# The end of a convolution, attention and expert kernel: a copy moved inside a merge, a last selection in another order, expert turns and output sums regrouped

## Chip, cores and metric

The kernel runs on one core of one Trainium2 chip. The metric is the device time of one execution in microseconds; all data are 32-bit floats. The program holds a fast path and a general path that is taken only when a check of value ranges fails; with the inputs used here the fast path alone is executed.

## The reference, cut to what matters

The input `x` has 4 images of 128 channels and 64 x 64 places. Layer 0 normalises groups of channels, takes three 1x1 convolutions with a leaky rectifier, and attends every place to every other (4096 x 4096 per image). Layer 1 sees the places as 4096 tokens of 128 features: a running-softmax attention with 8 heads, and then experts that choose their tokens.

```python
x = x + _L0_conv_ref(_gn(x), ...)            # layer 0
t = _to_tokens(x)
t = t + _L1_attn_ref(_ln_t(t), W_kv, q_proj) # running softmax over earlier tokens
t = t + _L1_ffn_ref(_ln_t(t), ...)           # 64 experts
x = _from_tokens(t, x)

def _L1_ffn_ref(x, gate_w, gate_b, weight1, weight2):
    logits = jnp.einsum('bsd,ed->bse', x, gate_w) + gate_b
    probs = jax.nn.softmax(logits, axis=1)               # over the tokens
    vals, idx = jax.lax.top_k(probs.transpose(0, 2, 1), 8)
    ...
    pooled = jnp.einsum('bked,bke->bed', gathered, topv) # 8 tokens per expert and image
    h = gelu(pooled @ weight1)                           # with a bias row
    out = h @ weight2                                    # with a bias row
    weighted = jnp.einsum('beo,bke->bkeo', out, topv)
    ...
    outputs = outputs.at[jnp.arange(Bn)[:, None], flat_idx].add(weighted)
```

For each image, each of the 64 experts picks the 8 tokens with the largest gate values; their weighted sum goes through the expert once, and the result is added to the same 8 tokens with the same weights. So the experts cannot start before the last token of an image has passed its gate.

## The kernel before

The residual stream lives in SBUF as `t`, with tokens on the partitions: 32 blocks of 512 tokens, 8 blocks per image. `layer0` does the convolutions and the large attention, `loop` the running attention in 32 steps, with a slot plan (`make_plan`) that places gate work between the matmuls of a step: slots 1, "V", 2, "W", "D", 3, 4, "O", "T", "G" in this order. The orders of TensorE, ScalarE (ACT), VectorE (DVE) and GpSimd (POOL) are as written in the program in this part; the DMAs that are named here are issued on SP's queue, the gathers on POOL's.

The change touches only the end of it.

**Last step of the loop (block 31).** `totals` forms sums over tokens in the PSUM tile `f_pt`; `close_totals` (L1166) copies it to SBUF on DVE; `outputs` (L1180) multiplies with that copy and adds to `t`. In slot "O", ahead of the last `totals` and of `close_totals`, the plan puts `merge_halves(3, 1)`, the first gather, `old_exps` and `root_table`. `merge_halves` (L1346) takes the best candidates of image 3 from the blocks done so far: values to the top 8, then for each of 4 ranks a comparison of places, a product with the row numbers and a sum (`f_rowf`), which becomes the row to gather. `root_table` (L1248) is a tiny square root that brings in ACT's table ahead of need.

**`last_choice` (L1514).** Block 31 alone is not yet in the choice. Its statistics, root, normalised rows (`f_x`), their transposes (`gate_turn`, `f_gtr`), logits (`f_pl`) and best 8 per half follow each other; then the new best are merged with the old top 8 (`f_pw1`, `f_merged`, `f_top`), exponentials are taken (`f_ce`, `chd`), the candidates are weighed and spread over experts (`weigh_candidates`, `spread_candidates`, `f_dd`), and TensorE sums into `f_pp`: four products with the gathered rows (L1576) and four with the tokens of block 31 (L1594), which need the transposed selection from `f_pc`. `f_pr` brings the divisors to every partition, and the last multiplication (L1605) fills `env.pooled`. Between these steps stand *fillers*: `fill(n, tag)` (L1467) transposes block `n` of `t` to PSUM, and `put_back(n, copy, count)` (L1480) copies it over the tokens in `t`, here always on ACT, since the output wants channels on partitions. Blocks 0 to 9 are turned in this way. The PSUM buffers go by tag: "kv" has two of two banks, "t", "o", "x" and "sm" one each.

**`experts` (L1700).** 64 experts in 16 groups of 4. For group `g`: `first(g)` (L1730) multiplies `env.pooled` by the first weights into `f_ph` and copies to `f_hr` on ACT; `turn(g)` (L1743) transposes that (`f_htr`, tag "sm"), adds the bias on DVE and takes the gelu on ACT into one of two `f_hs` tiles; `second(g)` (L1759) multiplies with the second weights into `f_eo`. As soon as `first` and `second` have read the weights of an expert, the DMA of a later expert into the same place is issued (`reload1`, L1672, and `reload2`, L1679). Beside it `turn_back(n)` (L1692) turns the remaining blocks of `t`. After 8 and 16 groups `spread` (L1775) takes the sums back to one row per expert and image: four products to one tile `f_pe` and four steps on DVE to `env.eo`.

**`stores` (L1814).** For two blocks at a time the outputs of the experts are spread over the tokens (`f_sct`, L1820), added to `t` on DVE, for every third pair with half of it on ACT and POOL, and written out, 512 KB at a time, the first and last pair in two parts of 256 KB.

Of the kernel before, what the change touches and what calls it, by code (L numbers as in the profile page):

```python
# [8 lines left out]
F32 = mybir.dt.float32  # L9
# [8 lines left out]
def conv_attn_hybrid_kernel(  # L18
# [809 lines left out]
    def fast():  # L828
# [418 lines left out]

        def root_table():  # L1248
            nc.scalar.activation(env.gnb[:, 0, 0:1], eps5, AF.Sqrt)
# [96 lines left out]
        def merge_halves(b, columns=4):  # L1346
# [16 lines left out]
            for h in range(2):  # L1363
                half = slice(h * E, (h + 1) * E)
                nc.vector.tensor_copy(own[half], first8[half, :, 4 * h : 4 * h + 4])
            hit = room[:, 4 * w : 12 * w].rearrange("p (k j) -> p k j", k=4)
# [147 lines left out]
        def last_choice():  # L1514
# [6 lines left out]
            fill(1, "kv", 1)  # L1521
            row_numbers(b, 1, 2)
# [9 lines left out]
            put_back(0, act, 2)  # L1532
# [42 lines left out]
            for kk in range(4):  # L1575
# [6 lines left out]
            )  # L1582
            ct = ex_at(1)[:, HB:].rearrange("p (j x) -> p j x", j=2)
# [8 lines left out]
            for h in range(2):  # L1592
# [5 lines left out]
                if h == 0:  # L1598
                    pr = ps.tile([P, BLK], F32, tag="t", name="f_pr3")
# [100 lines left out]
        def experts():  # L1700
# [74 lines left out]
            def spread(half, add):  # L1775
                pe = ps.tile([P, B, C], F32, tag="t", name=f"f_pe_{half}")
                for b in range(B):
                    at = 32 - 32 * half
                    nc.tensor.matmul(
                        pe[:, b, :], z_at[b][:, at : at + P], env.swap, start=True, stop=True,  # L1780
                    )
                for b in range(B):
                    nc.vector.scalar_tensor_tensor(
                        out=env.eo[:, b, :], in0=pe[:, b, :], scalar=env.den[:, b : b + 1],
# [29 lines left out]
        def stores():  # L1814
            for n in range(0, NB, 2):
                b, k = blocks[n]
                sc = ps.tile([P, 2, BLK], F32, tag="kv", name=f"f_sct_{n}", bufs=2)
                for h in range(2):
                    half = slice(h * E, (h + 1) * E)
                    nc.tensor.matmul(  # L1820
                        sc[:, h, :], env.eo[half, b, :],
                        env.lg[b][half, k : k + 2, :].rearrange("p k x -> p (k x)"),
                        start=True, stop=True,
                    )
                scv = sc.rearrange("p h (k x) -> p k h x", k=2)
                at = bass.ds(n * CPB, 2 * CPB)
                view = t[:, at, :].rearrange("p (k h c) x -> p k h (c x)", k=2, h=2)
                ends = n == 0 or n == NB - 2
                if n // 2 % 3 == 1:
                    part = env.rest.tile([P, 2, HB], F32, tag="xl", name=f"f_scs_{n}", bufs=3)  # L1830
                    nc.scalar.copy(part, scv[:, 0])
                    nc.gpsimd.tensor_tensor(view[:, 0], view[:, 0], part, ALU.add)
                    nc.vector.tensor_add(view[:, 1], view[:, 1], scv[:, 1])
                elif ends:
# [571 lines left out]
```

## Time and profile before

| | |
|---|---|
| runs shown | 2310.31, 2310.56, 2311.30 us (median 2310.56) |
| the profiled execution | 2303.66 us, of it 2301.8 us from first to last instruction |
| PE busy | 2238.5 us (97%) |
| DVE, ACT, POOL busy | 1447.1, 1092.2, 174.4 us |
| mean granted TensorE clock | 0.995 |
| read from HBM, written | 78.55 MB, 17.04 MB |
| start of `last_choice` on PE | about 2189.6 us after the start |
| start of `first(0)` | 2203.56 us |
| last group's `second` ends | about 2270.7 us |
| first store issued | 2274.57 us |

All positions in time are microseconds from the first instruction of the profiled execution. The durations of the profile belong to that one execution, which was shorter than the timed ones. "issue" in the chain of waits is time in which the engine that is on the chain waited for nothing that the profile shows. A matmul of 32-bit floats appears as two records, so counts of PE rows are twice those in the code where it isn't a transpose.

### The profile page before, as it was taken

Reading aid. Unit: us, or ns where it says so; the run is one execution under the profiler, and the core shown is the slowest. Engines: PE = TensorE matmul, PEld = TensorE weight load, DVE = VectorE, ACT = ScalarE, POOL = GpSimd, SP = SyncE. Lnnn points to the kernel's source line nnn. Section 1 sums busy time; section 2 is a strip of 40 time slices with the busy share of each in tenths; the row PEclk is TensorE's granted clock in tenths of the full one; section 3 lists DMA queues with packets and bytes.
Section 4 is the critical chain, followed back from the end, with each engine's and each line's share of the span. In section 5 each row is a group of like instructions: output and inputs, shape, how many; then the busy total and the mean of one; then the engine's idle time right before and its main releaser. Section 6 shows DMA issues by size and latency. Waiting matters only on the chain.

```text
span 2301.8 us, 43187 instructions
## 1 busy us (share of the span) xinstructions
PE 2238.5 (97%) x18352; PEld 1163.8 (51%) x18352; DVE 1447.1 (63%) x2380; ACT 1092.2 (47%) x1328; POOL 174.4 (8%) x380
## 2 busy tenths in 40 slices
PE   7999999999999999999999999999999999999997
PEld 3644444444444444444444444456556555566663
DVE  7666565655666565556555666667867777875643
ACT  2343334433333443344445554445566676565751
POOL 0000000000000000000000000011121121222311
PEclk9999999999999999999999999999999999999999
DMA  2000010000010000001000000020211211213488
GB/s 76 33 12 16 10 45 9 17 9 9 11 52 9 9 12 13 9 9 44 9 5 5 5 5 10 5 50 26 66 44 40 65 52 41 59 55 116 138 322 302
DMA packets 78555, 104.77 MB, mean 46 GB/s; under 512 B 8976, under 2 KB 44816, under 8 KB 78352
## 3 DMA queue, kind: packets, MB, share of 16 engines
q1 hardware_dynamic: 77264, 99.81, 13.9%
q8 instruction: 146, 2.39, 0.4%
q0 software_dynamic: 512, 1.05, 0.2%
q10 hardware_dynamic: 576, 1.05, 0.1%
q14 instruction: 57, 0.47, 0.1%
HBM read 78.55 MB, written 17.04 MB: 42 GB/s over the span
## 4 chain that ended last, share of the span: by engine, by line
PE 87%; DVE 6%; ACT 3%; DMA 2%; issue 1%; SPq 0%; POOL 0%; ACTq 0%; DVEq 0%; POOLq 0%
PE av L2009 37%; PE sc L1984 18%; PE f_pv L1128 9%; PE f_pk L973 8%; PE f_pt L1151 3%; PE f_po L1174 2%; PE pd L2035 1%; PE f_po L1186 1%; ACT f_e1a L980 1%; PE pa L1957 1%; DMA x<-in_x_dram 1%; PE pe L1931 1%; DVE f_e1a L981 1%; DVE f_e1a L982 1%; PE f_pl L1294 1%
## 5 line engine op out<-in xcount | busy, mean ns | idle before, releaser
L2009 PE MATMUL av<-pr,am 64*128 64x512 f32 x4096 | 977.7, 592 | 2.4 <-ACT pr L1989 2.4
L1989 ACT ACTIVATE pr<-sc 128x1024 f32<-128x1024 f32 x512 | 524.1, 1024 | 781.2 <-PE sc L1984 766.9
L1996 DVE TENSOR_TENSOR acc<-acc,pr 128x1024 f32<-128x1024 f32 x480 | 586.6, 1222 | 484.8 <-ACT pr L1989 480.5
L2009 PEld LDWEIGHTS av<-pr,am 64*128 64x128 f32 x4096 | 401.8, 187 | 472.9 <-issue 458.1
L1984 PE MATMUL sc<-e,e 64*128 64x512 f32 x2048 | 534.9, 591 | 3.3 <-DMA e<-side 3.3
L1984 PEld LDWEIGHTS sc<-e,e 64*128 64x128 f32 x2048 | 201.5, 187 | 234.7 <-issue 229.2
L1128 PE MATMUL f_pv<-f_held,f_ama 128*32 128x256 f32 x4096 | 237.5, 381 | 6.1 <-ACT f_e1a L980 5.1
L973 PE MATMUL f_pk<-f_held,f_ama 128*128 128x512 f32 x512 | 234.9, 603 | 0.0
L1133 ACT ACTIVATE f_amb<-f_pv 128x1024 f32<-128x1024 f32 x128 | 131.1, 1025 | 130.1 <-PE f_pv L1128 129.4
L981 DVE TENSOR_TENSOR f_e1a<-f_e1a,f_held 128x1024 f32<-128x1024 f32 x128 | 156.9, 1226 | 48.6 <-ACT f_e1a L980 48.3
L980 ACT ACTIVATE f_e1a<-f_pk 128x1024 f32<-128x1024 f32 x128 | 129.8, 1025 | 110.3 <-PE f_pk L973 56.1
L1128 PEld LDWEIGHTS f_pv<-f_held,f_ama 128*32 128x32 f32 x4096 | 129.2, 110 | 100.7 <-ACT f_e1a L980 11.9
L982 DVE TENSOR_REDUCE f_e1a<-f_e1a 128x8 f32<-128x1024 f32 x128 | 155.2, 1217 | 3.5
L973 PEld LDWEIGHTS f_pk<-f_held,f_ama 128*128 128x128 f32 x512 | 92.5, 190 | 108.3 <-issue 101.1
L1092 POOL COPY f_held<-f_e1a 32x32 f32<-32x32 f32 x128 | 30.7, 240 | 909.8 <-DVE f_e1a L1074 564.1
L1151 PE MATMUL f_pt<-f_amb,f_held 128*32 128x128 f32 x1920 | 83.2, 276 | 0.8 <-ACT f_amb L1133 0.8
L918 POOL MEMSET f_held<- 128x1024 f32 x1 | 1.0, 957 | 1036.6 <-DVE xn L1922 1036.6
L1151 PEld LDWEIGHTS f_pt<-f_amb,f_held 128*32 128x32 f32 x1920 | 60.0, 109 | 10.4 <-issue 5.2
L1192 DVE TENSOR_TENSOR t<-t,f_po 128x512 f32<-128x512 f32 (+1 forms) x33 | 22.1, 671 | 56.0 <-PE f_po L1186 56.0
L956 ACT ACTIVATE f_xl<-t,ln_nb,ln_rs 128x128 f32<-128x128 f32 x128 | 52.8, 491 | 0.8 <-PE pa L1957 0.8
L1275 ACT ACTIVATE f_x<-t,f_gnb,f_grs 128x128 f32<-128x128 f32 x122 | 49.7, 482 | 0.4 <-DVE f_gnb L1254 0.4
L1993 DVE COPY acc<-pr 128x1024 f32<-128x1024 f32 x32 | 22.2, 694 | 39.3 <-ACT pr L1989 39.3
(300 smaller groups left out, 1797.8 us busy)
## 6 DMA issues: line engine op xcount, KB each, us to landing
f_e2a<-f_rd SPq DMA_DIRECT2D x128, 128.0 KB, 2.9
xr<-in_xtok_dram SPq DMA_DIRECT2D x32, 256.0 KB, 3.0
f_table<-f_x SPq DMA_DIRECT2D x62, 128.0 KB, 2.0
out_dram<-t SPq DMA_DIRECT2D x14, 512.0 KB, 3.8
x<-in_x_dram SPq DMA_DIRECT2D x12, 512.0 KB, 6.4
e<-e SPq DMA_DIRECT2D x32, 128.0 KB, 2.2
f_ama<-f_rd SPq DMA_DIRECT2D x16, 256.0 KB, 3.8
f_e1b<-f_rd SPq DMA_DIRECT2D x16, 256.0 KB, 6.0
```

Of the source, the lines that this page charges most:

```text
L956: nc.scalar.activation(xl[:, c, :], t[:, b * NCH + i, :], AF.Identity, bias=ln_nb[:, b, i : i + 1], scale=ln_rs[:, b, i : i + 1],)
L973: nc.tensor.matmul(pk[:, i, :], xt_at(n)[:, bass.ts(c, P)], env.wks[:, bass.ts(i, BLK)], start=True, stop=True,)
L980: nc.scalar.activation(flat, pk.rearrange("p i x -> p (i x)"), AF.Silu)
L981: nc.vector.tensor_mul(ks, ks, env.qb)
L982: nc.vector.tensor_reduce(s[:, (n % GB) * CPB + c, :], ks, AX.X, ALU.add)
L1128: nc.tensor.matmul(pv[a * CH : (a + 1) * CH, i, :], xt_at(m)[:, bass.ts(c * NA + i, CH)], env.wvs[:, bass.ts(a, HH * C)], start=True, stop ...
L1133: nc.scalar.activation(env.amb[:, bass.ts(c, HD)], pv.rearrange("p i x -> p (i x)"), AF.Silu)
L1151: nc.tensor.matmul(env.pt[i * CH : (i + 1) * CH, :], lhs, rhs, start=i not in env.begun, stop=False, skip_group_check=True,)
L1984: nc.tensor.matmul(sc[:, u, :], e2[halves[u], p, :], e1[halves[u], cols], start=True, stop=True,)
L1989: nc.scalar.activation(pr, sc, AF.Exp)
L1996: nc.vector.tensor_add(acc, acc, pr)
L2009: nc.tensor.matmul(av, am[h, j, :], pr[h, u, :], start=(j == 0), stop=(j == NCH - 1))
```

## The change

1. The merge of slot "O" is cut in two: `merge_values` (up to the ranks' values and places) stays in "O", `merge_rows` and the first gather move to slot "T", behind `close_totals`.
2. In `last_choice`: the put-back of blocks 0 and 1 moves from behind `gate_norm` to the start. A new `exp_table`, a tiny exponential, follows the put-back of blocks 2 and 3; behind it stand the put-backs of blocks 4 and 5, which were after the exponentials. The filler of block 8 moves ahead of `f_pw1`, and blocks 10 and 11 become fillers too (tags "t" and "o"), put back where 4 and 5 were. `f_dd` is formed in two halves; the products with the gathered rows are cut in two pairs, the second behind `f_pc`; `f_pr` takes the last quarter of the tile of `f_pc`.
3. In `experts`: `turn(15)` moves ahead of `late_choice`, `turn_back` and `second` of group 14. Turning back starts with block 12, and two blocks per group are turned in groups 0 to 3 only (before: 0 to 5).
4. `spread` takes four tiles of 128 x 128 with the tags "t", "x", "sm", "t", and each product is followed by its step on DVE.
5. `stores`: for the first and the last pair the products are made per block (128 x 256, four of them) rather than per half (128 x 512, two).

```diff
+        def exp_table():
+            nc.scalar.activation(env.gnb[:, 0, 0:1], eps5, AF.Exp)
...
-        def merge_halves(b, columns=4):
+        def merge_halves(b):
+            merge_values(b)
+            merge_rows(b, 4)
+
+        def merge_values(b):
...
+            st["merge"] = (w, room, rows_)
+
+        def merge_rows(b, columns):
...
-        def spread_candidates(cw):
+        def spread_candidates(cw, parts=1):
             dd = ex_at(0)[:, : 4 * E].rearrange("p (k e) -> p k e", k=4)
-            nc.vector.tensor_tensor(
-                dd, env.pair[:, :E].unsqueeze(1).to_broadcast([P, 4, E]),
-                cw.unsqueeze(2).to_broadcast([P, 4, E]), ALU.mult,
-            )
+            m = 4 // parts
+            for i in range(parts):
+                nc.vector.tensor_tensor(
+                    dd[:, bass.ts(i, m)], env.pair[:, :E].unsqueeze(1).to_broadcast([P, m, E]),
+                    cw[:, bass.ts(i, m)].unsqueeze(2).to_broadcast([P, m, E]), ALU.mult,
+                )
             return dd
...
             fill(0, "kv")
             fill(1, "kv", 1)
+            put_back(0, act, 2)
             row_numbers(b, 1, 2)
             gathers(b, 1, 2)
             pool(B - 2)
...
             gathers(b, 2, 3)
-            put_back(0, act, 2)
             gate_turn(m, dve)
             row_numbers(b, 3, 4)
             gathers(b, 3, 4)
             put_back(2, act, 2)
+            exp_table()
+            put_back(4, act)
+            put_back(5, act)
             fill(6, "kv")
             gate_logits(m)
             fill(7, "kv", 1)
+            fill(8, "kv")
             late = st["cand"][:, bass.ts(k, 8)]
             pw = both_halves(late, "f_pw1")
-            fill(8, "kv")
             fill(9, "kv", 1)
+            fill(10, "t")
+            fill(11, "o")
...
             put_back(6, act, 2)
-            put_back(4, act)
             put_back(8, act, 2)
-            put_back(5, act)
-            dd = spread_candidates(weigh_candidates(b))
+            put_back(10, act)
+            put_back(11, act)
+            dd = spread_candidates(weigh_candidates(b), 2)
...
-            for kk in range(4):
+            for kk in range(2):
                 nc.tensor.matmul(pp, g_at(b, kk), dd[:, kk, :], start=(kk == 0), stop=False)
...
+            for kk in range(2, 4):
+                nc.tensor.matmul(pp, g_at(b, kk), dd[:, kk, :], start=False, stop=False)
...
-                    pr = ps.tile([P, BLK], F32, tag="t", name="f_pr3")
+                    pr = pc[:, 3 * P :]
...
             def spread(half, add):
-                pe = ps.tile([P, B, C], F32, tag="t", name=f"f_pe_{half}")
                 for b in range(B):
+                    pe = ps.tile([P, C], F32, tag=("t", "x", "sm", "t")[b], name=f"f_pe_{half}_{b}")
...
-            n = 10
+            n = 12
             for g in range(EG):
-                turn(g)
+                if g + 1 < EG:
+                    turn(g)
+                if g + 2 == EG:
+                    turn(g + 1)
                 late_choice(g)
-                for _ in range(2 if g < NB - 10 - EG else 1):
+                for _ in range(2 if g < NB - 12 - EG else 1):
...
+                if ends:
                     for i in range(2):
-                        nc.vector.tensor_add(view[:, i], view[:, i], scv[:, i])
+                        for h in range(2):
+                            half = slice(h * E, (h + 1) * E)
+                            nc.tensor.matmul(
+                                sc[:, h, bass.ts(i, HB)], env.eo[half, b, :],
+                                env.lg[b][half, k + i, :], start=True, stop=True,
+                            )
+                    view = t[:, at, :].rearrange("p (k h c) x -> p k h (c x)", k=2, h=2)
+                    for i in range(2):
+                        nc.vector.tensor_add(view[:, i], view[:, i], sc[:, :, bass.ts(i, HB)])
...
-            at(end, "O", merge_halves, B - 1, 1)
-            at(end, "O", gathers, B - 1, 0, 1)
+            at(end, "O", merge_values, B - 1)
+            at(end, "T", merge_rows, B - 1, 1)
+            at(end, "T", gathers, B - 1, 0, 1)
             at(end, "O", old_exps)
             at(end, "O", root_table)
```

More of the change, by code (lines that the diff above doesn't have):

```diff
@@ L1365, in merge_halves @@
                 nc.vector.tensor_copy(own[half], first8[half, :, 4 * h : 4 * h + 4])
+            st["merge"] = (w, room, rows_)
+        def merge_rows(b, columns):
+            st = sel[b]
+            own, top = st["own"], st["top"]
+            w, room, rows_ = st["merge"]
             hit = room[:, 4 * w : 12 * w].rearrange("p (k j) -> p k j", k=4)
@@ L1775, in spread @@
             def spread(half, add):
-                pe = ps.tile([P, B, C], F32, tag="t", name=f"f_pe_{half}")
                 for b in range(B):
+                    pe = ps.tile([P, C], F32, tag=("t", "x", "sm", "t")[b], name=f"f_pe_{half}_{b}")
                     at = 32 - 32 * half
                     nc.tensor.matmul(
-                        pe[:, b, :], z_at[b][:, at : at + P], env.swap, start=True, stop=True,
+                        pe, z_at[b][:, at : at + P], env.swap, start=True, stop=True,
                     )
-                for b in range(B):
                     nc.vector.scalar_tensor_tensor(
-                        out=env.eo[:, b, :], in0=pe[:, b, :], scalar=env.den[:, b : b + 1],
+                        out=env.eo[:, b, :], in0=pe, scalar=env.den[:, b : b + 1],
                         in1=add[:, b, :], op0=ALU.mult, op1=ALU.add,
@@ L1817, in stores @@
                 sc = ps.tile([P, 2, BLK], F32, tag="kv", name=f"f_sct_{n}", bufs=2)
[L1818 to L1825, printed above, removed]
-                at = bass.ds(n * CPB, 2 * CPB)
@@ L1827, in stores @@
[L1827 to L1834, printed above, removed]
-                    for i in range(2):
-                        nc.vector.tensor_add(view[:, i], view[:, i], scv[:, i])
-                else:
-                    nc.vector.tensor_add(view, view, scv)
+                ends = n == 0 or n == NB - 2
@@ new lines, in stores @@
+                at = bass.ds(n * CPB, 2 * CPB)
+                if ends:
+                    for i in range(2):
+                        for h in range(2):
[7 more added lines that the diff above has]
+                        nc.vector.tensor_add(view[:, i], view[:, i], sc[:, :, bass.ts(i, HB)])
+                else:
+                    for h in range(2):
+                        half = slice(h * E, (h + 1) * E)
+                        nc.tensor.matmul(
+                            sc[:, h, :], env.eo[half, b, :],
+                            env.lg[b][half, k : k + 2, :].rearrange("p k x -> p (k x)"),
+                            start=True, stop=True,
+                        )
+                    scv = sc.rearrange("p h (k x) -> p k h x", k=2)
+                    view = t[:, at, :].rearrange("p (k h c) x -> p k h (c x)", k=2, h=2)
+                    if n // 2 % 3 == 1:
+                        part = env.rest.tile([P, 2, HB], F32, tag="xl", name=f"f_scs_{n}", bufs=3)
+                        nc.scalar.copy(part, scv[:, 0])
+                        nc.gpsimd.tensor_tensor(view[:, 0], view[:, 0], part, ALU.add)
+                        nc.vector.tensor_add(view[:, 1], view[:, 1], scv[:, 1])
+                    else:
+                        nc.vector.tensor_add(view, view, scv)
```

## The prediction

> **What bounds the kernel now.** The page's slices come first: PE is busy in nearly all of them, but the change only touches the last 115 us, and there the DMA row rises to 8.
>
> ```profile
> PE   7999999999999999999999999999999999999997
> DMA  2000010000010000001000000020211211213488
> ```
>
> So I read the end by itself: the busy time of stretches cut where the DMA rate changes (columns: stretch, length, busy us of PE, PEld, DVE, ACT, POOL, then PE clock, DMA share, GB/s).
>
> ```profile
> 2184.00:2197.00 13.00, 10.88 (x196) 8.75 (x188) 7.44 (x35) 9.82 (x12) 3.79 (x4) 1.00 0.91 347
> 2197.00:2202.00 5.00, 3.34 (x32) 3.05 (x33) 2.82 (x14) 3.66 (x9) 0.00 (x0) 1.00 0.17 32
> 2203.50:2206.50 3.00, 2.94 (x16) 0.60 (x16) 0.00 (x1) 0.59 (x1) 0.00 (x0) 0.50 0.04 16
> 2206.50:2212.00 5.50, 5.50 (x61) 3.91 (x58) 2.88 (x9) 3.67 (x6) 0.28 (x2) 0.76 0.93 279
> 2212.00:2268.00 56.00, 51.60 (x694) 32.94 (x693) 12.60 (x37) 20.64 (x46) 4.19 (x25) 0.97 1.03 376
> 2268.00:2275.00 7.00, 5.52 (x56) 3.40 (x56) 2.82 (x8) 0.99 (x3) 0.00 (x0) 1.00 0.02 8
> 2282.00:2297.00 15.00, 9.60 (x36) 2.41 (x32) 9.98 (x11) 1.76 (x3) 3.82 (x3) 0.92 1.02 399
> ```
>
> The reader sees two full stretches of DMA and two empty ones. 2206.5 to 2268 is expert weights: 21 of the 64 experts are loaded ahead, and 43 x 512 KB = 22.5 MB follow, each load waiting until `first` or `second` has read the weights in its place. 2282 to 2297 is output. A stage that DMA fills moves as a whole with its first transfer; what PE and DVE do beside it costs nothing. So the time is set by the chain to the first reload (2205.50) and the chain from the last weights to the first stores. That is where I read the chain of waits (start, us, what):
>
> ```profile
> 2187.53 1.10 issue
> 2188.63 1.35 PE f_po L1186 x32
> ...
> 2194.96 0.66 PE f_etb L1476 x4
> 2195.62 0.61 PE f_pl L1294 x4
> ...
> 2198.78 0.79 issue
> 2199.57 1.08 PE f_pp L1576 x8
> 2200.65 0.23 PE f_pc L1579 x2
> ...
> 2201.51 0.66 PE f_pp L1594 x4
> ...
> 2203.56 3.64 PE f_ph L1735 x16
> ...
> 2271.04 1.17 PE f_pe L1779 x8
> 2272.24 0.36 DVE f_e1b L1783
> 2272.64 1.15 PE f_sct L1820 x4
> 2273.82 1.30 DVE t L1836 x2
> ```
>
> PE stands idle twice (1.10 and 0.79), and `first(0)` and `first(1)` take 3.64 where later pairs of groups take 2 x 1.00. The cause of the latter is the clock: cut at 3.41 us, it is 0.50 in 2202.33 to 2209.16 and 1.00 on both sides.
>
> [...] the changes at 2202.3, 2209.1, 2222.8 and 2226.2 lie 2, 4 and 1 windows of 3.41 apart, and a 128x32 by 512 f_ph matmul takes 1.06 slow, 0.62 fast. [...] The trace shows 1.28, and the ACTIVATE 0.01 later at 2186.39[...], so I use 1.28. [...] Here traffic ends at 2268.2 and PE gets the last weights at 2269.60, some 1.4 later.
>
> **The change, part by part.**
>
> *Totals copy inside the merge.* DVE copies f_pt (L1168) at 2188.24, behind five merge steps from 2187.13 on, while PE has ended its products at 2187.53. Moved ahead of those steps the copy runs 2187.13 to 2187.41; its matmuls ended at 2186.2. PE gains 2188.63 - 2187.55 = **1.08**, and the chain through t, statistics, root, norm and turn follows. POOL's first gather moves back behind the copy by 0.3; nobody reads it for 9 us. The other gathers follow DVE and are issued 1.1 earlier. SP has nothing in between but the bias load, also 1.1 earlier.
>
> *put_back(0) before the root.* Today it sits on ACT at 2193.92 to 2194.9, fill(6) waits for it, and f_pl stands behind fill(6) until 2195.62, though DVE has its input at 2195.23. After, the put-back uses ACT's idle time of 2.62 ahead of 2192.39: **0.33** more.
>
> *exp_table, put-backs 4 and 5.* Table load 1.28 + 0.20 + two 0.58 = 2.6 on ACT between the second put-back and f_ce. In the new timeline that is 2194.0 to 2196.6, f_ce is due at 2197.1: nothing, with 0.5 of cover. Now 10 and 11 take their place later: 3.0 of copies after f_bar, as before.
>
> *Fillers.* fill(8) stands ahead of f_pw: 0.55 of PE in a gap of about 0.5 (f_pl to f_pw), so 0 to 0.1 lost. fill(9), (10), (11) behind f_pw are 12 transposes x 0.137 = 1.64, against 1.04 + 0.79 idle today; f_pp becomes ready 1.7 after f_pw, so 0 to 0.1 lost. fill(10) and (11) newly wait for the put-backs of 4 and 5, due about 1 us earlier. Two turn_backs fewer in the experts lie under DMA: nothing.
>
> *f_dd in halves, f_pp split around f_pc.* lg ends 0.06 later on DVE, but f_pc no longer waits for all of f_pp: it ends at 2200.46 instead of 2201.01 (in today's clock of events), DVE copies ct in 0.43, and f_pp 2 and 3 (0.5) run under that copy. L1594 starts at 2200.97 rather than 2201.51: **0.54**. The third and fourth gathers land at 2198.9 and 2199.06 today, wanted at about 2199.2 after: no wait, but little room. f_pr in the free quarter of f_pc: nothing.
>
> Less 0.15 for the fillers, `first(0)` starts 1.08 + 0.33 + 0.54 - 0.15 = **1.8** earlier. The thin stretch between the last transposes and `first(0)`, today 2198.8 to 2203.56, shrinks to some 3 us, less than a window. If the clock stays full, L1594 and f_pr gain 0.3, and `first(0)`'s path to the first reload takes 1.2 instead of 1.94: 0.74. Unknown from both sides: 0 (dropped again, or not dropped in an ordinary run before) to 1.04; I take half, **0.5**.
>
> *Last turns sooner.* turn(15) moves ahead of second(14). f_htr(15) needs the one "sm" buffer, so PE waits for DVE's add of group 14 and second(14) starts at 2267.3, not 2266.59; second(15) then could start at 2268.65, not 2269.29. But the last f_e2b lands at 2269.60 and 29 of 32 f_eo follow it in both orders: **0**, cover 0.9.
>
> *spread in four tiles.* The first product ends at 2271.45 instead of 2272.20; DVE's first step (0.36) follows, then the fourth product, which waits for its buffer, and f_sct at 2272.15 instead of 2272.64: **0.45** (0.3 to 0.6). In group 8 the same wait is under DMA: a load issued takes 5.3 us to land.
>
> *Outputs' first sums.* In the built order of the changed program the first add of f_sct_0 carries a wait on PE and the second none, so the first already waits for all four matmuls. f_sct takes about 1.15 as now: **0**. Were it honoured for the first half alone, the first store would come 0.55 earlier, but the third store hangs on the copy and POOL's add, so at most 0.2 of that would last.
>
> Sum: 1.8 + 0.5 + 0.45 = 2.75. The profiled execution took 2303.66 (span 2301.8); after it 2300.9. The runs shown have a median of 2310.56, 6.9 above it; I subtract the same: **2307.8**.
>
> **Rivals.** (a) *The likeliest*, 2307.8, between 1.9 gained (clock no help, fillers dear) and 3.6: chance 0.60. (b) *A new wait takes the place of the old*: the gathers queue behind the initial loads, which fill DMA to 2197, and f_pp or the put-backs stall PE by about 1.5. For it: gathers took 5.4, 4.8 and 3.5 to land, ever shorter as DMA empties. Against it: three of four already land before their new use. Gain 1.2, 2309.4: 0.20. (c) *The ramp fills too*: 2206.5 to 2212 moves 279 GB/s where 376 follows; 5.5 x (1 - 279/376) = 1.4 more if a full clock frees the first places faster. With the full clock gain: 1.8 + 1.04 + 0.5 + 1.4 = 4.7, 2305.8: 0.17. (d) *Slower*: in-order PE stands at fill(10) or (11) because ACT reaches put-backs 4 and 5 late, behind the new table load, and f_ce behind them. It costs from about 1 us of lateness on, 1 for 1; to lose 0.2% it must be 1 + 2.75 + 4.6 = 8.4 late, three times what that ACT work lasts: 0.03. That the change doesn't do what it says holds for the outputs part and is in (a).
>
> **How the numbers follow.** 0.2% is 4.6 us, about what a measurement of this kernel can tell from no change. (a) and (b) lie within it; most of (c), 0.15, goes beyond; (d) 0.03 is slower. The range 2305.2 to 2309.9 takes in (a), most of (b) and (c).
>
> **What would show it.** Right: the matmuls of L1186 follow the products with no idle time, f_pl has no put-back before it, f_pc stands between two pairs of f_pp, the first reload comes near 2203, DMA traffic of the weights ends 1.8 to 2.9 earlier, f_sct 0.45 closer to the last f_eo, the first add still after four f_sct. Wrong: idle time ahead of the fills or f_pp, a clock of 0.50 as long as today's, or weight traffic that ends as late as now in spite of an earlier first reload.

## The result, and the profile after

The changed kernel took 2303.59 us, median of 17 runs (2300.78 to 2305.99). The kernel before, run beside it 14 more times, has now a median of 2306.64 over its 17 runs (2304.03 to 2311.30); without the three runs shown before it is 2306.11. The ratio is **0.9985, 95% interval 0.9978 to 0.9992**: 0.15% faster, clear of zero, but less than the 0.2% that the prediction took for the least that can be told from no change. The prediction said 2307.8, a gain of 2.75 us. The medians differ by 3.05. The gain was about right and the time was wrong, because the number that the gain was subtracted from was wrong.

The profiled executions of the two kernels are 2301.8 and 2301.6 us long. That is no contradiction. Both run the same instructions up to the first matmul of the last step's merge (`f_pw<-f_both`, L1325 before, L1328 after). I call its start **the mark**. Before reached it at 2185.23, after only at 2188.05, so 2.82 us were lost ahead of the change. From the mark to the end before took 116.57 us and after 113.55: 3.02 less (ends are taken from the span, which is given to 0.1 us). All steps below are read from the mark on.

Three of the stretches of before, moved by 2.82 us (columns as before: stretch, length, busy us of PE, PEld, DVE, ACT, POOL, then PE clock, DMA share, GB/s):

```profile
2186.82:2199.82 13.00, 12.42 (x216) 10.48 (x209) 8.45 (x41) 11.23 (x16) 3.78 (x4) 1.00 0.93 350
2199.82:2204.82 5.00, 4.31 (x36) 3.37 (x38) 2.49 (x10) 3.61 (x8) 0.00 (x0) 1.00 0.32 97
2206.32:2209.32 3.00, 3.00 (x51) 1.89 (x49) 2.52 (x8) 2.97 (x6) 0.00 (x0) 1.00 0.91 282
```

PE is busy for 12.42 of 13 us where it was for 10.88, and for 4.31 of 5 where it was for 3.34. In the third line the clock is 1.00 and the DMA share 0.91, where before showed 0.50 and 0.04: the reloads of the expert weights are already under way.

The chain of waits of after (start, us, what), its upper part:

```profile
2189.04 0.92 PE f_po L1174 x25
2189.97 0.29 DVE f_e1b L1168
...
2190.27 0.30 DVE f_e2b L1380
...
2191.25 0.15 DVE f_at L1397
2191.40 0.08 DVE f_src L1392
2191.48 0.01 issue
2191.48 0.75 DVE t L1192 x2
...
2200.44 0.22 issue
2200.66 0.63 PE f_pp L1596 x4
2201.29 0.36 PE f_pc L1599 x2
2201.65 0.12 PE f_pc L1600 x2
2201.77 0.53 PE f_pp L1604 x4
2202.30 0.65 PE f_pp L1616 x4
...
2203.65 0.28 DVE f_pooled L1627
2203.93 0.14 issue
2204.07 1.92 PE f_ph L1757 x16
```

The `issue` of 1.10 ahead of L1186 is gone. DVE copies the totals (L1168) first and does the merge's rows (L1380 to L1392) after it, and the add to `t` (L1192) follows these rows: DVE, not PE, is on the chain. It is nearly a draw, since PE's last `f_po` ended at 2191.43, 0.05 before the rows did. The gap ahead of `f_pp` is 0.22 where it was 0.79. `f_pc` stands between two pairs of `f_pp`. `first(0)` and `first(1)` take 1.92 where they took 3.64.

And its lower part:

```profile
2264.24 5.24 DMA f_e2b<-in_fw_dram
2269.48 0.04 issue
2269.53 1.07 PE f_eo L1786 x26
2270.60 0.02 issue
2270.62 0.30 DVE f_swap L1795
2270.93 0.14 issue
2271.06 1.39 PE f_pe L1801 x8
2272.45 1.09 PE f_sct L1848 x8
2273.54 0.02 issue
2273.57 1.30 DVE t L1854 x2
```

`f_pe` takes 1.39 (before 1.17), now with the DVE steps beside it, and the first add still comes behind all of the first `f_sct`.

### The profile page after: what moved, and what is told of

The parts are those of the page before. It is cut to its first block, busy times and chain, and to the rows that moved or that the text cites. A ratio compares the mean times of both kernels' runs of the same rounds, so it can differ in the third digit from the quotient of the medians.

```text
span 2301.6 us, 43208 instructions
## 1 busy us (share of the span) xinstructions
PE 2239.4 (97%) x18360; PEld 1165.2 (51%) x18360; DVE 1447.8 (63%) x2381; ACT 1091.6 (47%) x1329; POOL 174.0 (8%) x380
## 4 chain that ended last, share of the span: by engine, by line
PE 88%; DVE 5%; DMA 3%; ACT 3%; issue 1%; SPq 0%; ACTq 0%; DVEq 0%
PE av L2042 37%; PE sc L2017 19%; PE f_pv L1128 9%; PE f_pk L973 8%; PE f_pt L1151 3%; PE f_po L1174 2%; PE pd L2068 1%; PE f_po L1186 1%; PE pa L1990 1%; ACT f_e1a L980 1%; PE pe L1964 1%; DVE f_e1a L981 1%; DVE f_e1a L982 1%; DMA x<-in_x_dram 1%; PE f_pl L1297 1%
## 5 line engine op out<-in xcount | busy, mean ns | idle before, releaser
L1192 DVE TENSOR_TENSOR t<-t,f_po 128x512 f32<-128x512 f32 (+1 forms) x33 | 22.1, 671 | 54.5 <-PE f_po L1186 54.5
```

## Experiments

In each, "first(0)" is the start of its first `f_ph`, "reload" the issue of the first reload, "weights" the start of the first matmul on the last weights, all in us from the mark. In these traces all falls and rises of the granted clock of one execution lie whole multiples of 3.413 us apart. I call a stretch of that length, ending where the clock can so change, a clock window. Where the ends fall in the work, the phase, differs from one execution to the next: one lies 17.08 behind the mark in before, 16.39 in after. Most kernels have one profile. One profile holds the mechanism and an accident, the clock, so the steps count and not the totals.

| kernel | mark | first(0) | reload | weights | first f_sct | end | clock at first(0) |
|---|---|---|---|---|---|---|---|
| before | 2185.23 | 18.33 | 20.27 | 84.37 | 87.41 | 116.57 | 0.50 |
| before, again | 2188.75 | 18.01 | 19.95 | 85.01 | 88.06 | 117.05 | 0.50 |
| copy alone | 2189.04 | 18.46 | 20.41 | 84.60 | 87.65 | 116.76 | 0.50 |
| choice alone | 2187.15 | 17.13 | 19.05 | 82.34 | 85.39 | 114.45 | 0.50 |
| ends alone | 2188.66 | 19.73 | 21.68 | 84.53 | 87.39 | 116.44 | 0.50 |
| after | 2188.05 | 16.02 | 17.07 | 81.48 | 84.34 | 113.55 | 1.00 |
| after, again | 2186.21 | 16.36 | 17.41 | 80.41 | 83.27 | 112.59 | 1.00 |

### One part of the change at a time

*The copy alone* (a1_copy): the kernel before with

```diff
-            at(end, "O", merge_halves, B - 1, 1)
-            at(end, "O", gathers, B - 1, 0, 1)
+            at(end, "O", merge_values, B - 1)
+            at(end, "T", merge_rows, B - 1, 1)
+            at(end, "T", gathers, B - 1, 0, 1)
```

> The kernel before with part 1 alone: the merge cut in two, the copy of the totals between. Read from the last step's f_pw (before: at 2185.30) to the end, which took 116.50 before and 113.48 after; the time from f_pw to first(0) was 18.26 and 15.95, to the first reload 20.20 and 17.00. Theory (the chain to the first reload sets the start of a DMA stage that moves as a whole): the idle 1.1 before the outputs' matmuls goes, t's sums come 1.1 to 1.3 earlier and so does everything behind them: first(0) at 17.1, end at 115.3, with the clock falling where it fell before. Rival 1 (the gain sits in the experts and the stores): end stays at 116.4 to 116.6. Rival 2 (the gain is only where the clock's windows happened to fall): first(0) stays at 18.2.

*The choice alone* (a2_choice): the kernel before with all of the diff in `last_choice` and `spread_candidates`, `exp_table`, and `n = 12` in `experts`.

> The kernel before with part 2 alone (the order of the last choice, with blocks 10 and 11 as fillers). From f_pw of the last step. Theory: f_pl loses its wait for the put-back (0.26), the split f_pp gives 0.3 to 0.5, and the clock stays at 1.00 through first(0) and first(1), 0.4 on f_pp and 0.9 on the way to the first reload: first(0) at 17.2, first reload at 18.2, end at 114.7. Rival 1 (experts and stores): end at 116.4. Rival 2 (clock by chance): the clock falls to 0.50 under first(0) as before, reload at 19.6.

*The ends alone* (a3_ends): the kernel before with the diffs of `turn`, `spread` and `stores`.

> The kernel before with parts 3, 4 and 5 alone (last turns sooner, spread in four tiles, output products per block). Theory: the last weights land 84.3 after f_pw as before; from their landing to the first f_sct 2.8 to 2.9 instead of 3.04; end at 116.2. Rival 1 (the gain sits here): last weights or first store 1 to 3 earlier, end at 113.5 to 115.5.

The single timed runs were 2307.71, 2303.38 and 2306.82 beside 2303.92 for before. By what follows, one run of either kernel says nothing at this size, so I use the steps.

- First `f_pp`: 14.11 after the mark with the ends alone (which change nothing up to there), 13.00 with the copy, 13.72 with the choice, 12.61 in after. The copy is worth **1.11**, the choice's put-back and fillers **0.39**, and the two add up to 1.50.
- From the first `f_pp` to `f_pooled` at full clock: 3.00 with the choice, 2.99 in after, 3.30 in the kernel a4_busy below, which has the old order. Splitting `f_pp` around `f_pc` is worth **0.30**.
- From the weights' landing to the first `f_sct`: 3.04 in before, 3.05 with the copy or the choice, 2.86 with the ends and in after. `spread` in four tiles is worth **0.18**.

With the copy alone the gain of 1.11 was there at `f_pp` and gone at `first(0)`. Stretches of one clock window each:

```profile
2199.99:2203.40 3.41, 2.38 (x25) 2.02 (x23) 1.75 (x8) 2.48 (x7) 0.00 (x0) 1.00 0.30 106
2203.40:2206.81 3.41, 2.89 (x16) 2.81 (x15) 0.98 (x4) 1.28 (x2) 0.00 (x0) 0.50 0.53 159
```

The clock fell at 2203.40, 0.3 after the last two of `f_pp` had begun, so the matmuls behind it ran at a granted clock of 0.50. These two also waited for the last gather. PE's timeline of this kernel (in brackets the idle time before, and what ended it):

```profile
2203.11 0.46 PE L1586 MATMUL f_pp<-f_e2b,f_e1b 128*128 128x64 f32 x2 [0.22 <-DMA f_e1b<-f_table,f_at]
2203.38 0.62 PE L1589 MATMUL f_pc<-ident,f_lg 128*128 128x128 f32 x2
```

So `f_pp` to `f_pooled` took 5.1 us and not 3.3: 0.22 for the gather, the rest nearly all clock. The end expected at 115.3 came at 116.76. With the choice alone the clock fell just ahead of `first(0)`, so its reload came at 19.05 where 18.2 was expected. In the profile of before the clock fell later in the same chain (17.08 behind the mark, with the copy alone 14.36). A step gained, here 1.11 us, can be hidden by where the clock's window happens to end.

### What holds the clock

*Busy PE* (a4_busy): the kernel before with ten transposes of blocks 7, 8 and 9 done a second time, to the same place.

```diff
             fill(7, "kv", 1)
+            again(7)
...
             fill(9, "kv", 1)
+            again(8)
+            again(9, 2)
```

> The kernel before, with ten transposes of fillers 7, 8 and 9 made a second time (same data to the same place) where PE stood idle, ahead of f_pw1 and ahead of f_pp; nothing else moved. Theory (the thin stretch costs a clock window): PE's clock stays at 1.00 through first(0) and first(1); first(0) 0.2 to 0.4 earlier at 17.9 to 18.1, first reload 1.0 to 1.3 earlier at 19.0, end 1 earlier at 115.4. Rival (the clock falls by the window's phase, whatever PE does there): the clock falls, first reload at 20.2 or later, since the extra transposes can only delay.

`first(0)` came at 17.73 and the reload at 19.68. The clock was full up to 0.06 us before `first(0)` and then fell, for one window, so the expected 19.0 was missed. But the run does not test what it was made for: the last repeated transposes (L1487) end 0.3 us before the window begins that was followed by the fall.

```profile
2203.82 0.82 PE L1487 MATMUL f_etb<-ident,t 128*128 128x128 f32 x6
2204.94:2208.35 3.41, 2.60 (x22) 2.37 (x22) 1.51 (x7) 2.49 (x4) 0.00 (x0) 1.00 0.36 120
```

The second profile of before, without these transposes and with a window that ends 17.69 behind the mark (here 17.68), lost the clock for the same one window. What more work inside that window would do was not tried. This run serves as the old order at full clock: against its 17.73, after's 16.02 is 1.71 earlier. The time was 2308.78, one run.

*Fewer fillers* (b1_thin):

```diff
-            fill(10, "t")
-            fill(11, "o")
...
-            put_back(10, act)
-            put_back(11, act)
...
-            n = 12
+            n = 10
...
-                for _ in range(2 if g < NB - 12 - EG else 1):
+                for _ in range(2 if g < NB - 10 - EG else 1):
```

> The changed kernel without fillers 10 and 11 (8 transposes of about 0.137, 1.1 us of PE work behind f_pw1, and their put-backs on ACT; the two blocks are turned in the expert stage instead). All times from the first f_pw of the last step's merge on. Theory 'the fillers feed the clock': f_pp starts when f_dd is there, as before, so first(0) starts within 0.15 of the changed kernel's 16.0 us, but the window ahead of it holds 1.1 us less work and the clock is 0.50 at first(0), as in the kernel with the choice part alone; the first reload is issued at 18.0 instead of 17.1, and the end comes 0.5 to 1 later. Rival 'the phase of the window decides': the clock at first(0) is what this execution's phase gives; if it stays full the first reload comes at 17.1 without the fillers too and the end is the same within 0.2. Rival 'the fillers are in the way': first(0) 0.2 to 0.4 earlier. Median of timed runs within 1 us of the changed kernel's 2303.6 by all three.

`first(0)` came at 16.01, after's 16.02: the fillers cost PE nothing. The clock fell 0.16 after `first(0)` and the reload came at 17.77. That looks like the first theory. But the kernel b4_merge below has fillers 10 and 11, its window ended 0.18 after `first(0)`, and it fell all the same, with the reload at 17.78. One window before and after that moment, first in b4_merge and then in after:

```profile
2199.25:2202.66 3.41, 2.94 (x26) 2.61 (x29) 1.70 (x7) 2.60 (x4) 0.00 (x0) 1.00 0.17 48
2202.66:2206.07 3.41, 3.41 (x17) 0.67 (x10) 0.00 (x0) 0.59 (x1) 0.00 (x0) 0.50 0.48 177
```

```profile
2201.03:2204.44 3.41, 2.96 (x25) 2.45 (x28) 1.51 (x7) 2.40 (x4) 0.00 (x0) 1.00 0.31 80
2204.44:2207.85 3.41, 3.41 (x32) 1.76 (x28) 1.12 (x4) 2.31 (x3) 0.00 (x0) 1.00 0.65 229
```

The program is the same in this part and so is the busy time of PE (2.94 and 2.96), yet one clock fell and one did not. What differs is where the window ends, 0.37 behind the start of `first(0)` in after and 0.18 in b4_merge. So the phase can decide, and PE's busy share does not say which way. Median of b1_thin: 2305.49, 22 runs, ratio 0.9991 (0.9984 to 0.9997); its interval overlaps after's. Whether the fillers help to hold the clock, these profiles cannot tell, since fillers 10 and 11 lie ahead of the first `f_pp`, in the window before. The timed runs give a hint, below.

### The parts costed at nothing

*The last turn in its old place* (b2_turn), in the changed kernel:

```diff
-                if g + 1 < EG:
-                    turn(g)
-                if g + 2 == EG:
-                    turn(g + 1)
+                turn(g)
```

> The changed kernel with turn(15) back in its old place, in front of second(15) instead of second(14). The prediction's step ('0, the last f_e2b lands later than either order needs'): time from the last weights' landing to the first f_sct as in the changed kernel, 2.9 us within 0.1, and the end the same within 0.1 of it. Rival 'the earlier turn lets PE finish what does not wait for weights': first f_sct 0.3 to 0.6 later than in the changed kernel. Rival 'the turn costs': first f_sct 0.1 to 0.3 earlier, since PE does not wait for the one buffer in front of second(14). Median about 2303.6.

From the weights' landing to the first `f_sct` it took 2.79, after 2.86, and in after the last products start 0.05 behind the landing of the weights: the turn is worth nothing, as predicted. The median was 2302.61 (8 runs, ratio 0.9977, 0.9967 to 0.9987). The step read in the trace gives no reason for a gain; c_best below asks again.

*The two halves of the first and last sums in tiles of their own* (b3_halves), in the changed kernel:

```diff
+                if ends:
+                    parts = [
+                        ps.tile([P, 2, BLK], F32, tag="kv", name=f"f_scp_{n}_{i}", bufs=2)
+                        for i in range(2)
+                    ]
...
-                                sc[:, h, bass.ts(i, HB)], env.eo[half, b, :],
+                                parts[i][:, h, :HB], env.eo[half, b, :],
...
-                        nc.vector.tensor_add(view[:, i], view[:, i], sc[:, :, bass.ts(i, HB)])
+                        nc.vector.tensor_add(view[:, i], view[:, i], parts[i][:, :, :HB])
```

> The changed kernel with the two halves of the first and the last output step in two PSUM tiles instead of two halves of one tile. Theory (the prediction's step: in one tile the first add waits for all four matmuls, and the third store hangs on other work): with two tiles the first add starts after two of the four f_sct, so from the first f_sct to the first store is 1.4 us instead of 1.93, but from the first f_sct to the end stays 29.2 within 0.2, since the output stretch is filled by DMA and its later stores hang on ACT's copy and POOL's add. Rival 'the stretch moves with its first transfer': the end comes 0.5 earlier too. Rival 'the order on PE, not the tile, sets the add': the first store stays at 1.93. Median about 2303.6, or 0.5 less by the second.

Its chain:

```profile
2275.59 0.66 PE f_scp L1854 x4
2276.25 0.02 issue
2276.28 0.70 DVE t L1860
2276.97 0.04 issue
2277.01 1.15 PE f_sct L1864 x4
```

The add follows two of the four products, after 0.66 us where after's chain shows 1.09 of `f_sct`, and the first store is issued 1.51 us behind the first product (after 1.93). So the shared tile does set the wait, and not the order on PE; as each half takes 256 columns of both 512-column parts of that tile, the run does not tell the whole tile from its parts. But the end comes 29.88 us behind the first product, and 29.21 in after: 0.67 *later* (28.99 to 29.51 in the twelve other profiles). The two tiles take both "kv" buffers, the next pair's `f_sct` waits for an add and starts 1.49 behind the first product where it started 0.96 behind it, and the chain above goes on from there. An earlier first store brought nothing; an occupied buffer cost. Median 2305.59 (13 runs, ratio 0.9989, 0.9981 to 0.9997).

### The base: the same kernels again, and a stall ahead of the change

*Before, again* (c_before) and *after, again* (c_after), without an edit:

> The kernel before, once more, profiled again and timed again. Theory 'the clock's windows make the spread': the same instructions reach the first f_pw of the last merge anywhere in 2185 to 2191, each full-clock window lost before it (near 1484, 2134 and 2146) costing 1.5 to 2.2 us, and from there to the end takes 116 to 117 us, since the clock falls somewhere between the last f_pp and the first reload in every execution; median 2306 to 2307, timed runs spread over about 7 us. Rival 'before has a fixed base of 2310.5, and the profile shows a rare fast one' (what the prediction took): median near 2310, and few runs below 2306.

> The changed kernel, once more. Theory 'the clock's windows': first f_pw of the last merge anywhere in 2185 to 2191; first(0) 16.0 after it in every execution; the first reload 17.1 after it where the window's end falls more than 0.3 after first(0)'s start or more than 2.7 before it, else 17.8; the end 113 to 114.5 after it; median 2303 to 2304. Rival 'fillers hold the clock': the first reload 17.1 after it whatever the phase.

Before: 2306.35 (14 runs, 2302.75 to 2313.56), ratio to the kernel before on that chip 0.9997 (0.9988 to 1.0006). After: 2305.27 (14 runs, 2300.49 to 2309.40), ratio 0.9993 (0.9985 to 1.0001), a smaller gain than the first time, with overlapping intervals. Over all of them, 31 runs of after have a median of 2304.45 and 113 of before one of 2306.73: 2.3 apart. After's reload came at 17.41, since a wait for a gather appeared here too. PE's timeline of c_after:

```profile
2200.56 0.43 PE L1604 MATMUL f_pp<-f_e2b,f_e1b 128*128 128x64 f32 x2 [0.35 <-DMA f_e1b<-f_table,f_at]
```

that is 0.35 us, in one of two profiles of after. The gathers take 4.8 to 6.1 us to land in after and 5.3 to 6.1 in c_after, where before showed 3.5 to 5.4.

The timed runs tell how much of this is clock. Of 96 runs of before and the 31 of after the mean granted clock is on record, to three digits (median times in us, number of runs in brackets):

| mean clock | before | after |
|---|---|---|
| 0.993 | 2310.3 (6) | none |
| 0.994 | 2309.4 (13) | 2309.4 (1) |
| 0.995 | 2307.3 (33) | 2307.8 (3) |
| 0.996 | 2306.1 (23) | 2304.5 (13) |
| 0.997 | 2305.5 (16) | 2303.9 (12) |
| 0.998 | 2305.4 (5) | 2301.6 (2) |

Before alone spreads over 5 us with its clock. Where both have more than ten runs, after is 1.6 faster at equal clock, close to the 1.71 above. The rest of its gain goes with the clock: the mean over the runs is 0.9964 after and 0.9955 before. I estimate from these figures about 1.2 windows of 3.41 us at a clock of 0.50 fewer in each execution. The mean covers the whole execution, so it does not say where they were saved. The hint on the fillers: b1_thin's 22 runs have a mean of 0.9957, so that without the two fillers most of this is gone. The runs come from different comparisons, and at equal clock b1_thin is no slower than after, so it stays a hint.

The four add-ups of `t` (L1192) in blocks 26 to 29 mark equal work ahead of the change. Between the third and the fourth lies an idle time of PE in block NB-3, behind `f_pw` of `merge_halves(last)`. Its row in after:

```profile
2146.24 0.50 PE L1328 MATMUL f_pw<-f_both,ident 128*64 128x16 f32 x8 [2.56 <-DVE f_both L1341]
```

That stretch took 17.8 us in before and in c_after, 19.3 to 19.5 in five other kernels (after, a2, b1, b2, b3), and 20.7 to 20.8 in four (a1, a3, a4, c_before), with the same instructions in all eleven. In the first two the clock does not fall there, in the five it is down for one window, in the four for two. c_before:

```profile
2145.00:2148.40 3.40, 2.79 (x32) 1.60 (x36) 3.15 (x13) 0.00 (x0) 0.00 (x0) 0.50 0.13 34
2148.40:2151.80 3.40, 3.40 (x38) 2.10 (x30) 0.63 (x5) 1.87 (x4) 1.01 (x1) 0.50 0.22 67
```

c_before's mark stands 3.52 later than before's (2188.75, 2185.23); 2.9 of it are these two windows. So the profile of before, on which the prediction was built, was one of the lucky ones at this place.

These windows are not all. Ahead of the loop the fourteen profiles differ by more: DVE's first add to `t` in the loop came at 1545.64 to 1550.58 us, and from there to the add of block 27 all took 573.4 to 573.8. Eight of them lose a window near 1484 there, which costs 1.7 (from the first start to the last, the last eighth of layer 0's `av` matmuls takes 199.2 to 199.3 us with it and 197.6 without).

*The merge one slot later* (b4_merge in the changed kernel, x_merge_before in the one before):

```diff
-            at(NB - 3, 2, merge_halves, last)
+            at(NB - 3, 3, merge_halves, last)
```

> The changed kernel with the merge of the candidates of the batch before last's successor (merge_halves(last) in block NB-3) one slot later, 3 instead of 2. In both kernels PE stands idle there for about 2.5 us, its in-order queue behind f_pw that waits for DVE's selection, and in the changed kernel's execution the clock fell to 0.50 right after it (at 2146), in before's it did not. Theory 'a stall ahead of the change sets a part of the spread': with the slot later DVE has its selection done when PE comes to f_pw; the idle time goes (2.0 to 2.5 us), the clock does not fall at 2146, and the first f_pw of the last merge comes at 2183.5 to 2186.5 instead of 2185.2 to 2190.7; median 2300 to 2301.5, and the timed runs spread less than 5 us. Rival 'the wait moves on': what follows the merge (the gathers' row numbers, the next block's selection on DVE) is late by one slot and PE waits there: idle time of 1.5 to 2.5 us in slot 4 or in the next block, median 2303 to 2304. Rival 'the clock finds its next gap': idle time gone, gain 0.5 to 1.5, since a window falls at another place.

> The kernel before with the merge of batch 2 in block NB-3 one slot later (3 instead of 2), and nothing else. Theory 'a stall ahead of the change sets part of the base': PE's idle time of 2.56 in front of f_pw goes, and the clock does not fall near 2146; the last of the selection's four windows (from the t adds near 2138 to those near 2156) takes 15.8 instead of 17.8 without and 19.4 to 20.8 with a fallen clock; median 2.5 to 4 below the kernel before, so 2302.5 to 2304, as much as the whole change brings. Rival 'the gain in the changed kernel with this slot came from its other parts': less than 1 us.

PE's row in x_merge_before:

```profile
2149.97 0.41 PE L1325 MATMUL f_pw<-f_both,ident 128*64 128x16 f32 x8 [0.62 <-DVE f_lg L1298]
```

0.62 of idle time is left of 2.56, and what ends it is the step ahead of the merge. The clock does not fall there in any of the three profiles with the moved slot, and the stretch takes 15.8, 16.2 and 16.2. Their marks (2186.46 to 2187.13) are nevertheless no earlier than the earliest of the others, and b4_merge's lies at the late edge of what was expected: all three came late out of layer 0 (first add at 1550.03 to 1550.58). x_merge_before: 2304.05 (11 runs, ratio **0.9985**, 0.9976 to 0.9994): one digit brings as much as the change under study did in its first comparison. b4_merge: 2301.55 (7 runs, ratio 0.9973, 0.9962 to 0.9983). x_merge_before's own profile still lost three windows from 2201.64 on, and ended 118.67 behind its mark, the latest of all.

*Both* (c_best): the changed kernel with the merge one slot later and the turn in its old place.

> The changed kernel with the merge of batch 2 one slot later and turn(15) back in its old place. Theory (the two do not act on each other, and the turn is worth nothing): median 2300.5 to 2302, 4.5 to 6 below the kernel before; the last of the selection's four windows 15.8. Rival 'the turn's old place is worth the 1 us that its median showed': 2299.5 to 2300.5.

2301.29 (15 runs, 2297.92 to 2305.46), ratio to before **0.9970, 0.9961 to 0.9980**. Its interval lies below that of after in the same comparison (0.9985 to 1.0001). It is b4_merge's median within 0.3, so nothing is left of b2_turn's lower median, as far as intervals of some 2 us each way can tell.

## Why the prediction was right and wrong

**The step that failed: the base.** "The runs shown have a median of 2310.56, 6.9 above it; I subtract the same." The profiled 2303.66 and the median 2310.56 were taken for a fixed distance. Over all comparisons of many runs before ran 113 times: median 2306.73, from 2302.75 to 2313.56. Three of the 113 are as short as the profiled execution or shorter, and 13 as long as 2310.31 or longer. The profile came from the lower edge, the three runs shown from the upper: their distance is 6.9, that of the profile to the median of the 113 is 3.1. With 2306.64, the median of the 17 runs, the same sum gives 2306.64 - 2.75 = 2303.89; measured was 2303.59. The range had no width for the base at all, and its lower end, 2305.2, was above the result for that reason alone. The causes that are shown are windows lost near 2146 (up to 2.9 us) and near 1484 (1.7), within a difference of 5 us ahead of the loop that is not explained in full. That three runs in a row lay so high stays open; their clocks are not on record.

**The gain, step by step** (profiled pair, then what the experiments make of it):

| step | predicted | measured |
|---|---|---|
| totals copy | 1.08 | 1.34 in the pair, 1.11 with everything else the same |
| put_back(0), less the fillers | 0.33 - 0.15 | 0.39 |
| f_pp split, f_dd in halves | 0.54 | 0.30 |
| end of `f_pooled` to first(0) | 0 | -0.1 |
| first(0) at equal clock | 1.8 | 1.71 (1.99 against before, again, with its late add, see the end) |
| clock up to the first reload | 0.5 | 1.49 in the pair |
| weights' stretch, start to end | 0 | -0.31 in the pair, no trend in fourteen |
| spread | 0.45 | 0.18 |
| last turn; first sums | 0; 0 | 0; 0 |
| sum | 2.75 | 3.02 in the pair |

In the pair the reload came 20.27 - 17.07 = 3.20 earlier, of which 1.71 is order, 0.24 the late add of before and about 1.25 clock (the 1.49 of the table holds both); the stretch of weights gave 0.31 back (64.10 to 64.41), and 0.13 came between the weights and the stores and after. That 2.75 and 3.02 lie so close is in part luck. The prediction put the clock and the put-back too low and `f_pp`, `spread` and the stretch of weights too high, and these errors nearly cancel. The second pair, before again to after again, gives 4.46, of which 2.06 is the stretch of weights (65.06 to 63.00).

The premise that the weights move as a whole with their first transfer holds over the fourteen profiles: the first reload lies at 17.06 to 21.94, the stretch behind it takes 62.85 to 65.06 whatever the reload, and on a straight line through the fourteen a reload 1 us later goes with last weights 1.0 us later. But this scatter of 2.2 is nearly as large as the gain. That what PE and DVE do beside it costs nothing, no run tested by itself.

- *Totals copy*: right. DVE's rows now end as late as the products (2191.48 and 2191.43), a second bound that the prediction did not name.
- *Put-back and fillers*: the sum was 0.2 too low. The 0.15 put down for the fillers was nothing: without two of them `first(0)` comes at 16.01 and not earlier.
- *f_pp split*: a mis-sized term. By the prediction `f_pc` ends 0.54 + 0.36 = 0.90 behind the start of `f_pp`, and the copy `ct` (0.43) then covers the second pair (0.5). In after the first pair takes 0.63 and `f_pc` 0.36 + 0.12, in sum 1.11, and the second pair takes 0.53, so L1616 starts 1.64 behind the first `f_pp` where before's L1594 started 1.94 behind it: 0.30. The pieces are longer than their shares of the whole, 0.63 for 0.54 and 0.48 for 0.36.
- *Clock*: half of the 1.04 was too low in the pair, and about right over the timed runs, where 2.3 less 1.6 leaves 0.7. The hope for a full clock rested on the thin stretch shrinking to some 3 us, "less than a window". That the length of this stretch decides was an assumption and is not shown: the clock fell after windows in which PE was busy 2.05 to 2.96 of 3.41 us. The old choice lost the clock ahead of the first reload in all of before, c_before, x_merge_before, a3 and a4, for one window (a4, c_before) to three (a3, x_merge_before), with the reload at 19.68 to 21.93. The whole new choice and copy lost it in one of six profiles (b4_merge), for one window, with the reload at 17.06 to 17.78. Full clock was the ordinary case in these six, not one of two. The two groups met the window at different phases, though: in the first five a window ends 13.67 to 14.62 behind the mark, and in only one of the six (after, again, 13.68) does one end in that stretch. There the old order lost the clock (before, 13.67) and the new kept it. That the new order keeps it oftener rests on the timed runs' clocks, 0.9964 against 0.9955 over the whole execution.
- *Spread*: 0.18 and not 0.45. From the first product to the first `f_sct` it took 1.60 in before and 1.33 in after (2271.06 to 2272.39), where the prediction's times imply 1.11; and the first product comes 0.10 later behind `f_swap` (issue of 0.14, before 0.04). The fourth product got its buffer at 2271.97, and `f_sct` stood 0.42 behind it on PE.
- *Outputs' first sums*: right for the reason given. b3_halves got the earlier add, but paid for it with the second buffer; an earlier add without that price was not tried.
- *Landing of the last weights*: no price rests on it, but the reading of 1.4 us between the end of the traffic and PE is wrong. In before the last packets of the last load end at 2269.06, and PE starts on it at 2269.60, 0.54 later; from the last packet to the semaphore it is 0.42 to 0.49 in all fourteen profiles.
- *Table load*: the prediction's 1.28 is the `ACT_TABLE_LOAD` at 2185.10 in before (L1495), whose ACTIVATE starts at 2186.39. The load of `exp_table` in after took 1.28 too (2196.40), and ACT still stood idle for 0.82 ahead of `f_ce`: it cost nothing, as predicted.

Of the rivals, (b)'s wait for a gather was seen twice, in a1_copy at 0.22 and in c_after at 0.35, and not at 1.5 (the idle time of 0.15 at the same place in c_best has no releaser in its timeline): the prediction's "no wait, but little room" was close to the edge. (c)'s full clock came; its filled ramp did not: the first 10 us from the first reload on moved 287 GB/s before and 290 after. (d)'s late put-backs were not seen. The likeliest case, "between 1.9 gained and 3.6", holds the 3.05 of the first comparison, and misses the 1.8 of the second by a little (2307.04 to 2305.27, other medians on another occasion).

## What to carry to other kernels

Subtract a gain from the median of many runs, and give the range a width for the base: a profiled execution is one draw, and its distance to three runs is not a property of the kernel. Compare profiles from the last common instruction on, and at equal clock, since one lost window, 1.6 us near 2146, outweighs most of the steps in a change like this. When a run is to test what holds the clock, see that its extra work lies inside the window in question. Look for gaps of PE long before the place under work: moving one merge by one slot removed an idle time of 2 us and a fall of the clock that cost 1.6 to 2.9 in nine of eleven profiles.

## What the hardware showed beyond expectation

- The clock's window has a phase of its own in each execution (its end in the choice lies 17.08 behind the mark in before, 17.69 in before, again). For equal work, the mark lay between 2185.23 and 2190.99 in eleven profiles with the same instructions ahead of it. Windows lost near 2146 cost 1.6 us for one and 2.9 for two.
- Two windows of the same program with 2.94 and 2.96 us of PE busy time of 3.41 came out differently: a fall where 0.18 us of the dense `f_ph` matmuls was in it, none where 0.37 was. A window of c_best with 3.02 busy, which ended 0.71 ahead of `first(0)`, did not fall either, though the expectation of c_after would have had it fall. Busy time alone does not predict it: in the fourteen traces, from 150 us to 2205, 30 windows at full clock were followed by a fall, PE being busy 0.85 to 2.96 us in them, and 249 with no more than 2.96 kept the clock.
- An estimate that I made from the same traces afterwards separates them better. Take the moving columns of each PE record times its form's share of 128*128, the largest in the traces (128*64 128x16 counts 16 x 1/2), and add them up in each window. The 30 windows that were followed by a fall have at most 1509; of the 8381 that kept the clock one has 1437 and all others at least 1564. Of the two windows shown, b4_merge's has 1456 and after's 1565. It is no rule: in the expert stage, from 2216 on, some thirty windows with less than 1500 kept the clock.
- DVE's first add to `t` started about 0.3 us behind PE's last `f_po` (2189.71 to 2190.00) in all three profiles of kernels with before's order at this place and no edit behind it (before, c_before, x_merge_before), and 0.06 behind it in three kernels that differ from before only later (a2, a3, a4). The rows around it are the same; the trace does not show why. It is the 0.23 by which 1.34 exceeds 1.11.
